# A two-layer graph network on one Trainium2 core: entries of 72 more tiles of adj gathered into the memory of x's later rows

## The chip, the core and the metric

The kernel runs on one NeuronCore of a Trainium2 chip. PE (TensorE) multiplies matrices, DVE (VectorE) and ACT (ScalarE) work on tiles of 128 partitions, POOL (GpSimd) does a few such operations and issues the gathers, that is, the DMAs whose rows are picked by a list of indices, and SP (SyncE) issues most of the other DMAs. Each engine runs its own instructions in the order in which they were written; between engines they wait on semaphores. The metric is the device time of one execution in microseconds (us); lower is better. Before the change it is 1088.14 us, the median of 4 runs (1078.37 to 1096.14).

## The reference

`x` has 2708 rows of 256, `adj` is 2708 by 2708, sparse, with entries of 0 or between 0.05 and 1 and a full diagonal. Two layers, each followed by an addition of `x` and a layer norm over the 256:

```python
# layer 0; h = x, node_adj = edge_adj = adj without its diagonal, dn = de = diag(adj)
node_support = adj @ h
edge_output = gru_cell(node_support, h, edge weights)
for each of 3 heads:
    hW = h @ W
    hp, hm = (adj > 0) @ hW, (adj < 0) @ hW
    e_plus, e_minus = leaky_relu([hp, hm] @ a), leaky_relu([hm, hp] @ a)
    att = softmax over j of (e_plus[j] where adj > 0, e_minus[j] where adj < 0, else -9e15)
    edge_support += (att * adj) @ hW / 3
node_output = gru_cell(edge_support, h, node weights)
x = layernorm(x + de * edge_output + dn * node_output)
# layer 1: an attention of 4 heads over the entries with adj > 0.5
h = x @ W
e = leaky_relu(s_src + s_dst) where adj > 0.5, else -1e9
x = layernorm(x + softmax(e) applied to h + bias)
```

## The kernel before

Few entries of adj are not zero, so layer 0 does not multiply by all of it. The kernel has three phases, all written in `fast_path` (line 305).

*The scan (0 to about 250 us).* adj, transposed, is read once, in 6 groups of 512 columns by 11 pairs of blocks of 128 rows (lines 853 to 920). For each pair SP loads a tile `at2` (one of four), ACT takes signs, POOL multiplies the pair's diagonal block by `off_diag` (line 887) where the pair holds it, DVE reduces which rows have an entry in each strip of 64 columns (`f_found`), and PE sums signs. Between the pairs go one or more of the `later` loads (line 718), which bring weights, x and table columns, and PE's `keep` products, parts of the cells worked out early and stored to `XH`. When a group is through, `listed` and `spread` (lines 538 and 592) write with DVE, ACT and PE the lists `idx0` of the rows that have entries, 128 to a tile.

*Layer 0 (about 250 to 905 us).* The loop at line 1205 goes over `work0`, 181 tiles of 128 rows by 64 columns: 163 gathered by list and 18 whole ones. Of its tiles 0 to 59 belong to the first group of 512 nodes, 60 to 94 to the second, 95 to 125 to the third, 126 to 149 to the fourth, 150 to 173 to the fifth, the rest to the last, which has 148 nodes. For each tile

- `fetch_raw` (line 662) gathers its entries of adj, 64 floats for each of 128 rows. The first `EARLY` = 40 tiles go to memory that `m1`, the masks of layer 1, takes later; the others go round the 32 places of `rawp`, which lie in `home4` (profile name `f_home`; other rings have homes of the same name);
- `fetch_rows` (line 951) gathers the same rows of the table `T0`, x and the exponents beside it, into one of nine tiles `rows`;
- `prepared` (line 970) makes from both the weighted entries `four` (DVE, then ACT), and after every eighth tile (`RAWS`) DVE takes the least entry of the eight, `low`, out of the memory they were gathered to;
- `multiplied` (line 1002) and `divided` multiply on PE and divide.

After a group's last tile come `cells_and_norm` (line 1070): the products with `gat_w` into `side`, copied by ACT; the two cells; `back` (line 1134), which adds the result to `xn`, x's rows in memory (22 blocks of 256 floats to a partition); the norm; and the write of layer 1's table `T1`. `fetch_mask` (line 1198) gathers the 91 masks of layer 1 into one of six `raw` tiles and converts each on DVE into `f_m`; the calls stand ahead of tile 40 and run when their lists are there.

*Layer 1 (from about 905 us)* gathers rows of `T1` and applies the masks.

x comes into `xn` by three `later` loads of seven blocks and one of 20 rows, and `T0`'s columns of x are written from `xn` by four more.

The order on each engine isn't the order of the lines. `fast_path` runs against a `Plan` (line 97) that notes each instruction with what it depends on (by the memory it touches) and a cost, for a gather 1.25 us on POOL and 3.0 until it lands (`cost`, line 149). `issue` (line 226) then takes, for the engine that is free first, the ready instruction with the longest chain of costs behind it, and that is the order in which they are written out. A change of memory changes the dependencies, and with them the order on every engine. All notes are made in one helper, so the profile has one line for all of them, L215, and its tables are read by the tiles' names.

Of the kernel before, what the change touches and what calls it, by code (L numbers as in the profile page):

```python
# [10 lines left out]
F32 = mybir.dt.float32  # L11
# [9 lines left out]
P = 128  # L21
D = 256
# [19 lines left out]
W0 = 64  # L42
# [262 lines left out]
def fast_path(ctx: ExitStack, tc: tile.TileContext, i: dict, out: bass.AP, bad: bass.AP):  # L305
# [11 lines left out]
    nc = plan = Plan(tc.nc)  # L317
    x, xT_in, adj, adjT = i["x"], i["xT"], i["adj"], i["adjT"]
    N = x.shape[0]
    NB = (N + P - 1) // P  # L320
    NF = N // P
    size = [min(P, N - b * P) for b in range(NB)]
    last = NB - 1
    GR = CH // P
# [20 lines left out]
    const = ctx.enter_context(tc.tile_pool(name="f_const", bufs=1))  # L345
# [18 lines left out]
    T0 = dram.tile([N, TW], F32, name="f_T0")  # L364
# [11 lines left out]
    home3 = const.tile([P, 4 * CH], F32, name="f_home3")  # L376
    home4 = const.tile([P, 4 * CH], F32, name="f_home4")
# [68 lines left out]
    for t, of in ((less_room, TILES0 + TILES1), (less_whole, WHOLE0 + WHOLE1)):  # L446
        c = 0
        while c < len(of):
            e = c
# [40 lines left out]
    def on_every(src, wide):  # L490
        return bass.AP(tensor=src.tensor, offset=src.offset, ap=[[0, P], [1, wide]])
# [20 lines left out]
    xn = const.tile([P, NB, D], F32, name="f_xn")  # L512
# [19 lines left out]
    nc.gpsimd.memset(flags1, 0.0)  # L532
    m1 = const.tile([P, sum(TILES1), W1], U8, name="f_m1")
    small, lists = Rings(const, 2), Rings(const, 2)
    hotp, rawp = Rings(const, 2, home3), Rings(const, 32, home4)


    def listed(layer, batch, made):
# [109 lines left out]
    def gathered(dst, table, idx, at):  # L648
        nc.gpsimd.indirect_dma_start(
            dst, None, table, bass.IndirectOffsetOnAxis(ap=idx, axis=0), element_offset=at  # L650
        )
# [4 lines left out]
            of += [(c, True, b) for b in range(whole[c])] + [(c, False, t) for t in range(room_of[c])]  # L656
    raws = {}

    EARLY = 40
    early = m1.rearrange("p t w -> p (t w)").bitcast(F32)[:, : EARLY * W0]  # L660

    def fetch_raw(n):

        c, whole, m = work0[n]
        d0, w = spans[0][c]
        raws[n] = early[:, n * W0 : n * W0 + w] if n < EARLY else rawp.tile([P, W0], F32, name="raw")[:, :w]
        if whole:
            nc.sync.dma_start(raws[n], adjT[m * P : (m + 1) * P, d0 : d0 + w])
        else:
            gathered(raws[n], adjT, idx0[:, c, m : m + 1], d0)  # L670
# [47 lines left out]
    def later(dst, src):  # L718
        loads.append(lambda: nc.sync.dma_start(dst, src))

    def later_kd(src, wide, name):
        t = const.tile([P, KD, wide], F32, name=name)
        later(t, src.rearrange("(k p) n -> p k n", p=P))
        return t
# [1 line left out]
    cells = []  # L726
    of_cells = ("edge", "node")
    w_hs = [later_kd(i[f"L0_gnn_{cell}_WhhT"], 3 * D, f"f_{cell}_wh") for cell in of_cells]
    for b in range(0, NF, 7):
        e = min(b + 7, NF)  # L730
        later(xn[:, b:e, :], x[b * P : e * P, :].rearrange("(b p) d -> p b d", p=P))
    if NF < NB:
        later(xn[: size[NF], NF, :], x[NF * P :, :])
    for cell, w_h in zip(of_cells, w_hs):
        w_i = later_kd(i[f"L0_gnn_{cell}_WihT"], 3 * D, f"f_{cell}_wi")
        b_i = const.tile([P, 3 * KD], F32, name=f"f_{cell}_bi")
# [8 lines left out]
    bias_b = const.tile([P, D], F32, name="f_bias_b")  # L745
    for t, name in ((as_b, "a_src"), (ad_b, "a_dst"), (bias_b, "bias")):
        later(t, on_every(i[f"L1_gnn_{name}"], D))
    for b in range(0, NF, 7):
        e = min(b + 7, NF)
        later(T0[b * P : e * P, :D].rearrange("(b p) d -> p b d", p=P), xn[:, b:e, :])  # L750
    if NF < NB:
        later(T0[NF * P :, :D], xn[: size[NF], NF, :])
    later(
        diag[:, :NF].rearrange("p (b o) -> p b o", o=1),
        bass.AP(tensor=adj.tensor, offset=adj.offset, ap=[[N + 1, P], [P * (N + 1), NF], [1, 1]]),
# [97 lines left out]
    for g, cs in enumerate(groups):  # L853
        w = width[g]
        pe, pf = accs[0], dbs[0]
        c0, nf = base[g] // W0, w // W0
        for b0 in range(0, NB, 2):
# [25 lines left out]
            for b in pair:  # L883
                if b in cs:
                    p, o = size[b], b * P - base[g]
# [16 lines left out]
            for b in pair:  # L902
                p = size[b]
# [3 lines left out]
            for b in pair:  # L907
                p = size[b]
# [53 lines left out]
    def of_rows(n):  # L962

        c, whole, m = work0[n]
        if c == 0 and whole:
            return xn[:, m, :], Ew[:, m, :HEADS0], E3[:, m, :]
        r = rows[n]
        return r[:, :D], r[:, D : D + HEADS0], r.bitcast(BF16)[:, 2 * (D + HEADS0) : 2 * (D + HEADS0) + H3]

    def prepared(n):  # L970

        c, whole, m = work0[n]
        d0, w = spans[0][c]
        raw = raws.pop(n)
        four = sp.tile([P, 4 * W0], F32, name="four")
        a = four[:, :w]
        own = d0 - m * P
        if not whole:
            nc.vector.scalar_tensor_tensor(
                a, iota[:, :w], rel0[:, c, m : m + 1], raw, op0=ALU.not_equal, op1=ALU.mult  # L980
            )
        elif 0 <= own < P:
            nc.vector.tensor_mul(a, raw, off_diag[:, own : own + w])
        else:
            nc.vector.tensor_copy(a, raw)
        weight = of_rows(n)[1]
        for h in range(HEADS0):
            nc.scalar.activation(four[:, (h + 1) * w : (h + 2) * w], a, AF.Copy, scale=weight[:, h : h + 1])
        m0 = sp.tile([P, W0], BF16, name="m0", bufs=2 * COUNTED)
        nc.scalar.activation(m0[:, :w], a, AF.Sign)  # L990

        if n % RAWS == RAWS - 1 or n == len(work0) - 1:
            k = n - n % RAWS
            of, at = (early, k) if k < EARLY else (home4, (k - EARLY) % 32)
            nc.vector.tensor_reduce(
                low[:, k // RAWS : k // RAWS + 1], of[:, at * W0 : (at + n - k + 1) * W0], AX.X, ALU.min
            )
        ready[n] = (four, m0)
# [71 lines left out]
    def cells_and_norm(g):  # L1070
        c0, w = base[g], width[g]
        cc = slice(c0, c0 + w)
        sa, z = zs[g]
        bl = groups[g]
# [59 lines left out]
        def back(b):  # L1134
            p = size[b]
            pt = side()
            for o in range(KD):
                nc.tensor.transpose(
                    pt[:p, o * P : (o + 1) * P], total[:, o, b * P - c0 : b * P - c0 + p], ident
                )  # L1140
            y = xn[:p, b, :]
            nc.vector.scalar_tensor_tensor(y, pt[:p, :D], diag[:p, b : b + 1], y, op0=ALU.mult, op1=ALU.add)
            stats(y, p, b)
# [14 lines left out]
        def projected(b):  # L1158
            p = size[b]
            ph = side()  # L1160
            for k in range(KD):
                nc.tensor.matmul(
                    ph[:p, : D + 2 * HEADS1], lhsT=xT[:, k, b * P : b * P + p], rhs=w1[:, k, :],
                    start=(k == 0), stop=(k == KD - 1),
                )
            nc.vector.tensor_copy(s_d[:p, b, :], ph[:p, D : D + 2 * HEADS1])
            ah = gp.tile([P, TW], F32, name="ah", bufs=2)[:p]
            of_head = ah[:, :H65].rearrange("p (h c) -> p h c", h=HEADS1)
            s = small.tile([P, 2 * HEADS1], F32, name="s_d")[:p]
            nc.vector.tensor_scalar(s, ph[:p, D : D + 2 * HEADS1], REACH1, -REACH1, op0=ALU.min, op1=ALU.max)  # L1170
            nc.scalar.activation(of_head[:, :, C1 :], s[:, :HEADS1].rearrange("p (h o) -> p h o", o=1), AF.Exp)
            nc.scalar.activation(ah[:, H65:], s[:, :HEADS1], AF.Exp, scale=SLOPE - 1.0)
            nc.tensor.transpose(pd[:HEADS1, b * P - c0 : b * P - c0 + p], s[:, HEADS1:], ident[:p, :p])
            nc.vector.tensor_mul(
                of_head[:, :, :C1], ph[:p, :D].rearrange("p (h c) -> p h c", h=HEADS1),
                of_head[:, :, C1:].to_broadcast([p, HEADS1, C1]),
            )
            nc.sync.dma_start(T1[b * P : b * P + p, :], ah)
        for b in bl:
            back(b)  # L1180
        rstds(bl)
# [4 lines left out]
        for b in bl:  # L1186
            projected(b)
# [17 lines left out]
    for n, (c, whole, m) in enumerate(work0):  # L1205
        if n == EARLY:
            for k in slot1:
                fetch_mask(k)
        fetch_raw(n)
        fetch_rows(n)  # L1210
        prepared(n)
        if multiplied(n):
            divided(c)
            d0, w = spans[0][c]
            if d0 + w in (base[g] + width[g] for g in range(NG)):
                cells_and_norm(d0 // CH)
# [140 lines left out]
def tile_adj_resnorm(tc: tile.TileContext, i: dict, out: bass.AP):  # L1357
    nc = tc.nc
    with tc.tile_pool(name="guard", bufs=1) as gp:
        bad = gp.tile([P, 1], F32, name="bad")  # L1360
        fast_path(tc, i, out, bad)
        with tc.tile_pool(name="guard_ps", bufs=1, space=PSUM) as ps:
            one = gp.tile([P, 1], F32, name="guard_ones")
            nc.vector.memset(one, 1.0)
            nc.vector.tensor_scalar(bad, bad, 0.0, None, op0=ALU.is_gt)
            n = ps.tile([1, 1], F32, name="n_bad")
            nc.tensor.matmul(n, lhsT=bad, rhs=one, start=True, stop=True)
            flag = gp.tile([1, 1], I32, name="flag")
            nc.vector.tensor_copy(flag, n)
        taken = nc.values_load(flag[0:1, 0:1], min_val=0, max_val=P)  # L1370
        with tc.If(taken > 0):
            general_path(tc, i, out)
# [436 lines left out]
```

## Time and profile before

| | |
|---|---|
| four runs, median | 1088.14 us |
| lowest, highest | 1078.37, 1096.14 us |
| profiled execution, its own time | 1079.45 us |
| its span, first to last instruction | 1077.4 us |
| busy: PE, DVE, ACT, POOL | 847.0 (79%), 616.4 (57%), 534.4 (50%), 521.5 us (48%) |
| mean granted clock of PE | 0.876 |
| DMA queues: hardware (SP), software (POOL), hardware (ACT) | 21.6%, 16.8%, 3.5% of 16 engines' span |

In the profile, a group of instructions is told by engine, operation and `out<-in` with the program's names. The number after `x` is how many there are, then busy time and the mean of one, then how long the engine stood idle before them and what ended most of that. The waits list for each engine what it waited for: us in total, times, the longest one. Busy shares are means over three phases with different limits, so the phase of a number matters. A gather counts as busy on POOL while POOL writes its descriptors, some 0.95 us; its data land later. The shares of the clock are of PE's full speed, as the throttle granted them.

### The profile page before, as it was taken

The page shows a single profiled execution, that of the slowest core. Times are in us where ns is not written, and L with a number is a line of the kernel's source. Part 1 is how long each engine was busy: PE and PEld are TensorE (multiplying, and loading weights), DVE is VectorE, ACT ScalarE, POOL GpSimd, SP SyncE. Part 2 cuts the span into 40 slices and gives each one's busy share as a digit, 9 for nine tenths or more (in the row PEclk, how much of TensorE's full clock was granted, in tenths as well). Part 3 has the DMA queues.
Part 4 walks back from the last instruction along what each step waited for, and adds up shares of the span by engine and source line. Part 5 has one row for each costly group of instructions (what it writes and reads, how often), then busy time and mean ns, then how long its engine had stood idle before and what let it go on. Part 6 is the DMA issues. An engine that isn't in the chain of part 4 may idle for free.

```text
span 1077.4 us, 13865 instructions
## 1 busy us (share of the span) xinstructions
PE 847.0 (79%) x3879; PEld 517.4 (48%) x3879; DVE 616.4 (57%) x2011; ACT 534.4 (50%) x1499; POOL 521.5 (48%) x613
## 2 busy tenths in 40 slices
PE   5983888898888777778977766988758886887783
PEld 3431333344666335553554335535523474776672
DVE  5772658842564248653753365347513545788897
ACT  4783778874777326562564244434602242034354
POOL 2054653003656737666765556466473301666650
PEclk9996979999988879799987988888888986899996
DMA  8983968764333224332533142232221101444433
GB/s 300 305 261 106 271 210 265 208 179 154 97 87 87 51 57 130 82 76 62 167 109 92 28 148 77 63 98 65 75 60 27 43 26 60 124 140 146 147 106 108
DMA packets 84302, 131.94 MB, mean 122 GB/s; under 512 B 21368, under 2 KB 43136, under 8 KB 83576
## 3 DMA queue, kind: packets, MB, share of 16 engines
q1 hardware_dynamic: 56056, 71.21, 21.6%
q0 software_dynamic: 20320, 45.59, 16.8%
q10 hardware_dynamic: 7840, 14.16, 3.5%
q8 instruction: 33, 0.54, 0.2%
q14 instruction: 53, 0.43, 0.1%
HBM read 109.79 MB, written 21.12 MB: 122 GB/s over the span
## 4 chain that ended last, share of the span: by engine, by line
PE 27%; DVE 11%; another core or an unknown queue 6%; issue 5%; ACT 2%; DMA 1%; POOL 0%; SPq 0%; DVEq 0%; POOLq 0%; ACTq 0%
PE side L215 14%; PE acc L215 9%; DVE f_home L215 7%; PE db L215 4%; DVE f_xn L215 2%; ACT four L215 1%; DVE st L215 1%; ACT f_home L215 1%; DMA rows<-f_T,f_idx 1%; DVE four L215 1%; DVE rden L215 0%; DVE rden_own L215 0%; DVE f_m L215 0%; ACT L215 0%
## 5 line engine op out<-in xcount | busy, mean ns | idle before, releaser
L215 POOL DMA_INDIRECT rows<-f_T,f_idx x254 | 254.4, 1002 | 254.8 <-issue 107.3
L215 PE MATMUL acc<-four,rows 128*128 128x256 f32 (+1 forms) x712 | 210.2, 439 | 15.1 <-ACT four L215 8.7
L215 PEld LDWEIGHTS acc<-four,rows 128*128 128x128 f32 x712 | 146.1, 217 | 56.2 <-issue 15.9
L215 ACT ACTIVATE four<-four,rows 128x64 f32<-128x64 f32 (+1 forms) x534 | 145.6, 336 | 40.7 <-DMA rows<-f_T,f_idx 12.1
L215 POOL DMA_INDIRECT f_home<-in_adjT_dram,f_idx x130 | 127.3, 979 | 57.0 <-issue 33.3
L215 POOL DMA_INDIRECT raw<-in_adj_dram,f_idx x91 | 89.4, 982 | 64.2 <-DVE f_m L215 39.6
L215 PE MATMUL acc<-f_home,rows 128*65 128x128 f32 (+1 forms) x480 | 68.1, 297 | 22.7 <-DVE f_home L215 18.7
L215 ACT ACTIVATE f_home<-f_home,f_minus_half 128x1024 bf16<-128x1024 f32 (+4 forms) x72 | 69.8, 976 | 26.1 <-remote 15.2
L215 DVE TENSOR_REDUCE f_found<-f_home 128x16 f32<-128x1024 f32 (+5 forms) x84 | 71.8, 883 | 16.0 <-DMA f_home<-in_adjT_dram 8.9
L215 PE MATMUL side<-f_home,f_edge_wi 128*128 128x512 f32 (+1 forms) x144 | 65.5, 597 | 19.4 <-DVE f_home L215 10.9
L215 DVE TENSOR_TENSOR f_home<-f_home,side 128x512 f32<-128x512 f32 (+1 forms) x56 | 36.7, 657 | 67.0 <-PE side L215 43.7
L215 ACT ACTIVATE f_home<-f_home 128x1024 bf16<-128x1024 f32 (+4 forms) x72 | 63.0, 882 | 17.8 <-PE acc L215 7.1
L215 PEld LDWEIGHTS acc<-f_home,rows 128*65 128x65 f32 x480 | 56.4, 149 | 30.9 <-DVE f_home L215 22.6
L215 DVE SCALAR_TENSOR_TENSOR four<-f_iota,f_rel,f_home 128x64 f32<-128x64 f32 (+1 forms) x130 | 35.6, 279 | 61.3 <-PE acc L215 22.9
L215 PE MATMUL side<-f_home,f_node_wi 128*128 128x512 f32 (+1 forms) x144 | 64.1, 580 | 4.8 <-DVE f_home L215 4.7
L215 PE MATMUL db<-f_home,f_only 128*22 128x512 bf16 (+2 forms) x132 | 40.7, 389 | 29.8 <-ACT f_home L215 26.6
L215 DVE SCALAR_TENSOR_TENSOR f_home<-pl,rows,f_m 128x128 f32<-128x128 f32 x196 | 55.0, 344 | 14.6 <-PE acc L215 5.7
L215 PE MATMUL side<-f_home,f_gat_w 128*128 128x512 f32 (+1 forms) x144 | 59.9, 575 | 1.5 <-DVE f_home L215 1.2
L215 PE MATMUL db<-f_home,rows 128*65 128x128 f32 x376 | 52.8, 291 | 7.3 <-DVE f_home L215 4.2
L215 PEld LDWEIGHTS side<-f_home,f_edge_wi 128*128 128x128 f32 x144 | 27.7, 205 | 53.3 <-issue 37.0
L215 ACT ACTIVATE m<-four 128x64 bf16<-128x64 f32 (+1 forms) x181 | 40.7, 246 | 19.0 <-DVE four L215 13.1
L215 PEld LDWEIGHTS db<-f_home,rows 128*65 128x65 f32 x376 | 43.5, 146 | 12.6 <-DVE f_home L215 6.7
(207 smaller groups left out, 1415.9 us busy)
## 6 DMA issues: line engine op xcount, KB each, us to landing
f_home<-in_adjT_dram SPq DMA_DIRECT2D x50, 512.0 KB
f_XH<-kept ACTq DMA_DIRECT2D x48, 256.0 KB
f_home<-f_XH SPq DMA_DIRECT2D x48, 256.0 KB
f_home<-f_TS SPq DMA_DIRECT2D x5, 1024.0 KB
rows<-f_T SPq DMA_DIRECT2D x31, 132.0 KB
rows<-f_T,f_idx POOLq DMA_INDIRECT x254
f_T<-f_home SPq DMA_DIRECT2D x21, 132.0 KB
f_xn<-in_x_dram SPq DMA_DIRECT2D x3, 896.0 KB
```

The source lines that it names most:

```text
L215: call = lambda: f(*args, **kwargs)
```

## The change

The ring `rawp` goes. A tile's entries now have a home by their number: the first 40 as before, the next 72 in `soon`, which is the memory of `xn`'s blocks 4 to 21 (18 blocks of 256 floats are 72 places of 64), and the others in turn in the 32 places of `home4`. The reduction `low` reads from the same home.

At the start only `xn`'s first four blocks are loaded; x's rows of the other groups are loaded in `cells_and_norm`, ahead of `back`, by SP (four loads of four blocks; for the last group one of a block and one of 20 rows). `T0`'s columns of x are copied from x in DRAM and no longer from `xn`.

```diff
-    hotp, rawp = Rings(const, 2, home3), Rings(const, 32, home4)
+    hotp = Rings(const, 2, home3)
...
-    EARLY = 40
+
+    EARLY, NEXT = 40, (NB - GR) * D // W0
     early = m1.rearrange("p t w -> p (t w)").bitcast(F32)[:, : EARLY * W0]
+    soon = xn[:, GR:, :].rearrange("p b d -> p (b d)")
+
+    def raw_home(n):
+
+        if n < EARLY:
+            return early, n
+        if n < EARLY + NEXT:
+            return soon, n - EARLY
+        return home4, (n - EARLY - NEXT) % 32
 
     def fetch_raw(n):
 
         c, whole, m = work0[n]
         d0, w = spans[0][c]
-        raws[n] = early[:, n * W0 : n * W0 + w] if n < EARLY else rawp.tile([P, W0], F32, name="raw")[:, :w]
+        home, at = raw_home(n)
+        raws[n] = home[:, at * W0 : at * W0 + w]
...
-    for b in range(0, NF, 7):
-        e = min(b + 7, NF)
-        later(xn[:, b:e, :], x[b * P : e * P, :].rearrange("(b p) d -> p b d", p=P))
-    if NF < NB:
-        later(xn[: size[NF], NF, :], x[NF * P :, :])
+    later(xn[:, :GR, :], x[: GR * P, :].rearrange("(b p) d -> p b d", p=P))
...
-    for b in range(0, NF, 7):
-        e = min(b + 7, NF)
-        later(T0[b * P : e * P, :D].rearrange("(b p) d -> p b d", p=P), xn[:, b:e, :])
-    if NF < NB:
-        later(T0[NF * P :, :D], xn[: size[NF], NF, :])
+    for b in range(0, NB, 7):
+        e = min((b + 7) * P, N)
+        later(T0[b * P : e, :D], x[b * P : e, :])
...
-            of, at = (early, k) if k < EARLY else (home4, (k - EARLY) % 32)
+            of, at = raw_home(k)
...
+        if g > 0:
+            full = [b for b in bl if size[b] == P]
+            if full:
+                nc.sync.dma_start(
+                    xn[:, full[0] : full[-1] + 1, :],
+                    x[full[0] * P : (full[-1] + 1) * P, :].rearrange("(b p) d -> p b d", p=P),
+                )
+            if len(full) < len(bl):
+                nc.sync.dma_start(xn[: size[last], last, :], x[last * P :, :])
         for b in bl:
             back(b)
```

## The prediction

> **What bounds the kernel now.** I read the page's chain first, then its groups, the waits by stage, the busy time by windows, and last the instructions around the longest gaps.
>
> ```profile
> PE 27%; DVE 11%; another core or an unknown queue 6%; issue 5%; ACT 2%; DMA 1%; POOL 0%; SPq 0%; DVEq 0%; POOLq 0%; ACTq 0%
> ...
> L215 POOL DMA_INDIRECT rows<-f_T,f_idx x254 | 254.4, 1002 | 254.8 <-issue 107.3
> ...
> L215 POOL DMA_INDIRECT f_home<-in_adjT_dram,f_idx x130 | 127.3, 979 | 57.0 <-issue 33.3
> L215 POOL DMA_INDIRECT raw<-in_adj_dram,f_idx x91 | 89.4, 982 | 64.2 <-DVE f_m L215 39.6
> ```
>
> PE leads the chain and POOL has 0% of it: the engine whose work this change moves is not the bound. POOL's work is gathers of about 0.98 us plus 0.30 us between two of them, 1.25 us each. The 130 into `f_home` and 33 into `f_m` are the entries of adj (the change concerns the 130), 91 into `raw` the masks of layer 1.
>
> Who waits for entries in layer 0 (250 to 905 us), by the waits of DVE, then of ACT:
>
> ```profile
> DVE f_low L215 <- DMA f_home<-in_adjT_dram,f_idx: 23.8, 4, 9.6
> ...
> DVE f_m L215 <- DMA raw<-in_adj_dram,f_idx: 21.6, 18, 3.4
> ```
>
> ```profile
> ACT four L215 <- DMA rows<-f_T,f_idx: 12.1, 12, 2.5
> ```
>
> The four `f_low` waits end at about 365.9, 497.1, 595.3 and 697.5 us. The last three lie in the gat_w products of a group's cells, where PE is busy without a break (10.0 of 10 us from 490, 590 and 690). They cost PE nothing.
>
> Then the windows. Columns: length, busy us (instructions) of PE, PE's weight loads, DVE, ACT, POOL, then PE's granted clock, DMA share and GB/s.
>
> ```profile
> 63.80:78.00 14.20, 10.91 (x62) 4.13 (x59) 9.74 (x14) 12.40 (x17) 11.10 (x11) 0.88 0.95 306
> 78.00:95.40 17.40, 3.68 (x22) 1.59 (x19) 0.00 (x0) 2.18 (x3) 13.17 (x14) 0.75 0.35 87
> 120.70:150.80 30.10, 24.53 (x81) 10.03 (x80) 20.92 (x41) 22.37 (x30) 23.64 (x22) 0.78 0.78 234
> 171.50:204.20 32.70, 29.56 (x139) 12.54 (x138) 27.62 (x56) 29.19 (x42) 0.00 (x0) 0.99 0.87 273
> 213.70:240.60 26.90, 26.90 (x123) 12.64 (x121) 13.40 (x40) 21.48 (x49) 0.00 (x0) 0.95 0.56 156
> ...
> 366.60:383.10 16.50, 8.07 (x17) 3.31 (x16) 0.03 (x1) 1.87 (x2) 12.54 (x14) 0.81 0.16 26
> ...
> 795.50:811.10 15.60, 0.01 (x1) 0.00 (x0) 1.15 (x5) 0.62 (x2) 8.45 (x9) 0.64 0.19 42
> ```
>
> Lines four and five: POOL has two empty stretches in the scan, 32.7 and 26.9 us. Lines two, six and seven: every engine but POOL nearly stands still. All three lie in the second half of a long unbroken train of gathers: 25 from 63.8 to 95.4, 24 from 352.7 to 383.1, 23 from 778.0 to 806.4. PE's longest gaps there are 17.9, 8.4 and 15.6 us. But 22 gathers from 120.7 to 150.8 (line three) cost PE only 2.8 us. Why such trains stop PE, the trace does not tell; that they go together is all I use. The third, on PE:
>
> ```profile
> 793.63 1.88 PE L215 MATMUL side<-f_home,f_edge_wi 128*128 128x512 f32 x4
> 811.10 3.78 PE L215 MATMUL side<-f_xT,f_edge_wh 128*128 128x512 f32 x4 [15.59 <-ACT f_home L215]
> ```
>
> The last line for later is on POOL, the first gather of T's rows after the last off_diag multiply:
>
> ```profile
> 240.63 0.63 POOL L215 TENSOR_TENSOR f_home<-f_home,f_off_diag 128x128 f32<-128x128 f32 x2 [26.96 <-ACT f_home L215]
> 250.53 0.98 POOL L215 DMA_INDIRECT rows<-f_T,f_idx  x1 [9.27 <-issue]
> ```
>
> **The change part by part.** All gathers stay (163 of entries, 91 masks, 254 of rows); the planner's order moves. I counted it in the two programs, on POOL.
>
> *Ahead of the first gather of rows:* 61 gathers of entries before, 108 after. 47 more at 1.25 us are 58.8 us; the two empty stretches hold 59.6 us. The lists decide when they can run. In the trace group 1's list is written at 158.3 and 164.5 us, group 2's at 195.2 and 202.9. After the change 26 gathers, which need no list later than group 1's, stand in one train between group 3's multiplies by off_diag (167.9 us) and group 4's first: 170.5 + 26 x 1.25 = 203 us, and that multiply ran at 205.7. Covered. Then 25 more stand between group 4's second multiply (212.8) and group 5's, for group 2's list: 213.7 + 25 x 1.25 = 245.0 us, where that multiply was ready at 240.6. PE's last products and the logits that the rows need queue behind it: **+4.4 us** on the path (nothing, if the 9.3 us before the first row gather swallow it; +10 if the lists slip by 5 us).
>
> *Trains in the scan.* The 26 and the 25 are two new unbroken trains. Price of one: from 2.8 us (the 22 at 120.7) to 17.9 us (the 25 at 63.8). By length they are nearest the second, by place and by work (a running scan whose lists of group 0 are done) nearest the first; I take the place: 2 x 2.8 = **+5.6 us**, bounds 0 and 35.8.
>
> *In the tile stretches of layer 0.* Up to the 150th gather of rows POOL has 102 gathers of entries and 43 masks before, 55 and 90 after: 145 against 145. The masks fill the room at once, so the stretches get no relief: ACT's 12.1 us for rows and the trains of 16 to 20 in the cells of groups 0 to 2 stay. 0 us, bounds -12.1 and +12.1. DVE's 23.8 us are worth 0 as shown; DVE will next wait there for masks (`f_m`, 21.6 us today).
>
> *Behind the 150th gather of rows* stood the other 48 masks; now one does. The train of 23 with 18 masks at 778.0 is gone, and with it, by my reading, the stop of PE: 15.6 us. What is late next there is ACT's copy of `side`, ready when the products end at 792. In the 5.9 us after the gap the clock was 0.5, so that work takes some 3 us less: **-18.6 us**, bounds -18.6 and 0.
>
> The clock row agrees with the Trainium skill, "TensorE: Matmul & The Clock Gate", section "Part 1: The HAM clock gate", that an idle window of about 3.4 us halves PE's clock; by that page's figure alone the regained work would be worth about half of one such window, 1.7 us, in place of my 3.
>
> *Loads of x.* Early on four loads (2.7 MB) become one of 0.5 MB, and T0's columns come from x directly: 2.25 MB less, at 304 GB/s (0 to 50 us) 7.4 us of DMA time. The 47 gathers read 47 x 32 KB = 1.5 MB more in the scan, in 16 packets of 2 KB and about 0.15 us each: 47 x 0.15 = 7.1 us over 16 engines. They balance: 0, bounds -7 and +7. T0's writes are complete by my reading well before 250 us.
>
> Six loads of xn (0.5 MB; 1.7 us at 304 GB/s, 4.3 us at the 122 GB/s of the whole span) enter SP's queue. They stand far ahead of the `back` that reads them; each waits for DVE's last read of those entries, and queued behind it are whole rows of T0, loads of XH and writes of T1. Had every one held its group by 4.3 us it would be 5 x 4.3 = 21 us; a group's cells last some 40 us, so I take 0.
>
> DVE: the same reductions `f_low`, six of them earlier, 0.68 us each, each behind eight landings. In the scan they stand in front of work on lists, but their gathers stand earlier still: 0, bounds 0 and 6 x 2.4 = 14 us (2.4 being the shortest such wait).
>
> One rule speaks against gathering beside a busy DVE. In 112 to 171 us DVE was busy two thirds of the time and gathers still took 0.94 us mostly, 0.97 to 0.98 in the mean, 2.38 at most. The Trainium skill, "SBUF — State Buffer", section "SBUF: two separate sides", says that POOL cannot write descriptors while DVE runs certain copies; from its 620 ns that become 3100 ns, an estimate for 47 gathers would be 47 x 2.5 = 117 us lost. The row decides: 0.
>
> Sum: 4.4 + 5.6 - 18.6 = **-8.6 us**. The profiled execution took 1079.45 us (span 1077.4), so 1070.9. It lies 8.7 us below the median 1088.14 of runs from 1078 to 1096; the same step from the median gives 1079.5. If the stops vary from run to run, the removed one is part of what separates them; I take a bit under the middle, **1074 us**.
>
> **The rivals.**
>
> *A. The stop at 778 goes and the scan stays whole (forecast).* 1070.9 less ACT's 12.1 and the 5.6 of the new trains, 1053, up to 1077. Chance 0.38.
>
> *B. The stop moves.* The masks that made the train of 23 now stand in trains of 17 to 20 in the cells of groups 0 to 3; before, such trains cost PE 8.4 (24), 4.1 (20), 3.3 (18), 2.4 (17). If three of them gain 6 each, the 18.6 are given back: 1088 + (4.4 + 5.6 + 18 - 18.6) = 1097, or about 1079 if none does. It says also that the promised relief does not happen, for which the count 145 against 145 speaks. 1077 to 1099. Chance 0.30.
>
> *C. Slower: the dense scan stops.* Place: the trains of 26 and 25, 170 to 245 us, where PE is at 29.6 of 32.7 and 26.9 of 26.9 us, so every microsecond counts. Price: 17.9 each as at 78 us, 35.8, + 4.4, and the stop at 778 returns half: 1079.45 + 35.8 + 4.4 - 9 = 1110.6. It decides from a total of 30 us of PE gap between 170 and 250. For it: length of train. Against it: 22 gathers at 120 to 150. Chance 0.32.
>
> **How the numbers follow.** About 1% is what a measurement of this kernel can tell from no change. A is faster by over 1% (below 1077), B within, C slower (above 1099): 0.38, 0.30, 0.32. A's own range is 1053 to 1077. The range for 8 in 10 takes A, B, and C to a little over its price: 1053 to 1112. Out of it are a scan that loses more than C's price, and gains from several terms at once.
>
> **What would show it.** Right: between 780 and 815 us no PE gap over 5 us, at most one mask behind row gather 150; POOL busy in 171 to 245; PE still at 27 and more of 30 us there; the first gather of rows at 250 to 257 us. Wrong: PE gaps over 8 us in 180 to 245 (C); new gaps of 8 us and more beside mask trains at 370 to 720 (B); `back` waiting for DMA of `f_xn`; POOL gathers with a mean over 1.1 us. Should the first row gather come before 245 us, the loads of x were worth more than I gave them; should it come after 265, the lists slipped.

## The result and the profile after

The changed kernel takes 1088.92 us (median of 10 runs, 1082.83 to 1097.28), the kernel before 1085.21 us in 15 runs taken with it (1066.75 to 1096.14). Ratios, here and below, leave out executions more than 1.5% above the fastest of the same kernel (nine of the 15 before), and three profiles of the experiments (loads alone, pauses in two places, pauses without the order) fell on such executions, so their rows are given but not compared closely. The ratio is 1.0152, 95% interval 1.0098 to 1.0206, while the two medians differ by 0.3%: the change makes the kernel no faster, and by the ratio some 1.5% slower. Its profiled execution took 1087.88 us (span 1086.1), against 1079.45 (1077.4).

The busy time by windows, as it was read before (length, then busy us of PE, its weight loads, DVE, ACT and POOL with instructions, PE's granted clock, DMA share, GB/s), now around the trains of gathers of the changed kernel (a train is an unbroken sequence of gathers on POOL):

```profile
68.30:85.60 17.30, 14.21 (x76) 5.59 (x72) 9.70 (x14) 13.19 (x18) 13.34 (x14) 0.90 0.89 263
85.60:106.40 20.80, 0.04 (x1) 0.08 (x1) 1.86 (x3) 2.68 (x4) 10.57 (x12) 0.62 0.14 27
...
175.60:198.70 23.10, 21.56 (x86) 8.62 (x86) 18.29 (x43) 18.58 (x23) 18.35 (x18) 0.93 0.94 259
198.70:209.30 10.60, 0.00 (x0) 0.00 (x0) 2.94 (x3) 3.26 (x4) 7.86 (x10) 0.71 0.40 92
230.10:251.70 21.60, 20.70 (x82) 9.08 (x80) 14.32 (x39) 13.66 (x25) 16.86 (x18) 1.00 0.64 181
251.70:263.30 11.60, 0.04 (x1) 0.09 (x1) 0.92 (x5) 0.93 (x2) 8.31 (x9) 0.61 0.23 53
...
824.10:839.70 15.60, 15.60 (x37) 6.84 (x36) 3.52 (x5) 3.10 (x6) 0.00 (x0) 1.00 0.00 0
```

Each pair of lines is one train: first all engines work, then nearly only POOL does. The train of 25 from 68.3 us was there before and stops PE for 20.8 us (17.9 before). The two new ones, from 175.6 and from 230.1 us, stop it for 10.6 and 11.6 us. The last line is the place in the program where PE stood still before, 13.8 to 29.4 us after the 163rd gather of rows (which came at 781.7 us before and comes at 810.3 now): PE works all of its 15.6 us, and POOL has nothing to do.

The waits of PE in the scan (50 to 262 us) put the same in one line, first of the kernel before, then of the changed one:

```profile
PE db L215 <- ACT f_home L215: 18.3, 2, 17.9
```

```profile
PE db L215 <- ACT f_home L215: 37.5, 5, 20.8
```

(Only waits that end by 262 us are in it, so the last gap isn't.) The end of the scan, on POOL:

```profile
276.94 0.98 POOL L215 TENSOR_TENSOR f_home<-f_home,f_off_diag 128x128 f32<-128x128 f32 x2 [14.49 <-ACT f_home L215]
287.23 0.98 POOL L215 DMA_INDIRECT rows<-f_T,f_idx  x1 [9.31 <-DMA f_T<-f_Ew]
```

The first gather of rows comes at 287.2 us and not at 250.5. So the balance, from the gathers of rows in the two profiles, is:

| stretch | before | after | difference |
|---|---|---|---|
| start to the 1st gather of rows (scan) | 250.5 | 287.2 | +36.7 |
| 1st to 163rd (tiles and cells of layer 0) | 531.2 | 523.1 | -8.1 |
| 163rd to 164th (end of layer 0) | 127.5 | 107.7 | -19.7 |
| 164th to the end of the span (layer 1) | 168.2 | 168.0 | -0.2 |

The sum is +8.7, the difference of the spans. The gathers themselves hardly changed:

```profile
L215 POOL DMA_INDIRECT f_home<-in_adjT_dram,f_idx x67 | 63.5, 948 | 27.1 <-issue 17.5
L215 POOL DMA_INDIRECT f_xn<-in_adjT_dram,f_idx x63 | 63.7, 1010 | 25.5 <-issue 17.9
```

The mean of one is 948 and 1010 ns where it was 979. The question is what made the scan 37 us longer.

### The profile page after: what moved, and what is told of

It is laid out like the page before. It is cut to its first block, busy times and chain, and to the rows that moved or that the text cites. A ratio compares the mean times of both kernels' runs of the same rounds, so it can differ in the third digit from the quotient of the medians.

```text
span 1086.1 us, 13831 instructions
## 1 busy us (share of the span) xinstructions
PE 843.7 (78%) x3879; PEld 513.4 (47%) x3879; DVE 612.7 (56%) x2011; ACT 535.9 (49%) x1499; POOL 528.7 (49%) x613
## 5 line engine op out<-in xcount | busy, mean ns | idle before, releaser
L215 POOL DMA_INDIRECT rows<-f_T,f_idx x254 | 258.7, 1018 | 293.7 <-issue 146.8
L215 PE MATMUL acc<-four,rows 128*128 128x256 f32 (+1 forms) x712 | 206.3, 433 | 31.8 <-ACT four L215 19.5
L215 PEld LDWEIGHTS acc<-four,rows 128*128 128x128 f32 x712 | 142.9, 213 | 73.7 <-ACT four L215 25.4
L215 POOL DMA_INDIRECT raw<-in_adj_dram,f_idx x91 | 93.0, 1021 | 57.5 <-DVE f_m L215 32.7
L215 POOL DMA_INDIRECT f_home<-in_adjT_dram,f_idx x67 | 63.5, 948 | 27.1 <-issue 17.5
L215 POOL DMA_INDIRECT f_xn<-in_adjT_dram,f_idx x63 | 63.7, 1010 | 25.5 <-issue 17.9
L215 PE MATMUL side<-f_home,f_node_wi 128*128 128x512 f32 (+1 forms) x144 | 60.0, 548 | 1.5 <-DVE f_home L215 1.4
L215 PE MATMUL side<-f_home,f_gat_w 128*128 128x512 f32 (+1 forms) x144 | 57.3, 555 | 1.2 <-DVE f_home L215 1.2
L215 PE MATMUL db<-f_home,rows 128*65 128x128 f32 x376 | 48.4, 278 | 5.8 <-DVE f_home L215 5.5
L215 PE MATMUL acc<-f_home,f_home 128*9 128x512 bf16 (+2 forms) x132 | 42.2, 404 | 10.3 <-ACT f_home L215 9.4
```

Source lines behind the costliest of these rows:

```text
L215: call = lambda: f(*args, **kwargs)
```

## The experiments

Three causes are at hand for the scan: the new loads of x, the gathers' place in POOL's queue (the multiplies by `off_diag` behind them), and the stop of the other engines while a long train runs. "Gathers ahead" below counts gathers of entries in front of the first gather of rows.

**The loads of x alone** (`e1_loads`): the kernel before with the change's early load of four blocks, the copies into T0 and the late loads, but with the ring.

```diff
-        later(xn[:, b:e, :], x[b * P : e * P, :].rearrange("(b p) d -> p b d", p=P))
...
+    later(xn[:, :GR, :], x[: GR * P, :].rearrange("(b p) d -> p b d", p=P))
...
+        later(T0[b * P : e, :D], x[b * P : e, :])
...
+        if g > 0:
+            full = [b for b in bl if size[b] == P]
```

> The kernel before with only the change's loads of x: the first four blocks of xn early, the others ahead of back, T0's columns copied from x. The ring of 32 places stays, so 61 gathers of entries stand ahead of the first gather of rows as before. Theory (the long trains of gathers stop the scan): the first gather of rows comes within 5 us of the 250.5 us of before, the ratio to the kernel before is 0.99 to 1.01, and the stop at 778 is still there. Rival (the loads of x slow the scan, for which the first list came 4.5 us later in the changed kernel): the first gather of rows comes after 262 us and the ratio is 1.01 or more.

Measured: 1082.40 us against 1083.16, ratio 1.0025 (0.9973 to 1.0078). By the time, the loads cost nothing that can be told (the interval ends at +0.8%, some 8 us). The stop behind the 163rd gather of rows is still there, with a PE gap of 14.4 us. In the profile the first gather of rows came at 263.6 us, past the 262 that was to speak for the loads; the next run, which has the loads too, decides.

**The gathers held until the scan is over** (`e2_hold`):

```diff
+    nc.vector.tensor_copy(
+        soon.rearrange("p (n w) -> p n w", w=W0)[:, :, :1],
+        found0[:, len(TILES0) - 1, NB - 1 :].rearrange("p (n o) -> p n o", o=1).to_broadcast([P, NEXT, 1]),
+    )
     for n, (c, whole, m) in enumerate(work0):
```

> The changed kernel in which a DVE copy of 72 elements, which needs the last group's found rows, stands ahead of the gathers into xn's later rows, so that they can't run in the scan: 48 gathers of entries stand ahead of the first gather of rows (108 in the changed kernel). Theory (trains): the first gather of rows comes at 240 to 256 us where the changed kernel has 287; the gathers come back in layer 0, which takes as long as before or longer, and the masks stand at its end again; ratio to the kernel before 0.99 to 1.015. Rival (the loads of x): the first gather of rows stays after 270 us.

Measured: first gather of rows at 250.2 us, time 1087.14, ratio 1.0079 (1.0038 to 1.0121). With the loads of x in place and the gathers out of the scan, the 37 us are gone. They came with the gathers. Layer 0 (1st to 164th gather of rows) then takes 661.2 us, as long as before (658.7) and longer than in the changed kernel (630.8), as expected: a train of 25 in a group's cells stops PE for 16.9 us at 496.8.

**Pauses in the trains of the scan** (`e3_fill`). POOL multiplies a spare tile six times after every fourth gather in a row. The planner counts the time, so the order changes a little.

```diff
             for call in op.calls:
                 call()
+            if e == "gpsimd":
+                run = run + 1 if op.method == "indirect_dma_start" else 0
...
+                rows += op.out.startswith("rows")
+                if run >= 4 and rows == 0:
+                    run, free[e] = 0, free[e] + 2.4000000000000004
+                    for _ in range(6):
+                        self.fill()
...
+    spare = const.tile([P, 100], F32, name="f_spare")
...
+    plan.fill = lambda: tc.nc.gpsimd.tensor_mul(spare, spare, spare)
```

> The changed kernel in which, until the first gather of rows, POOL does six small multiplies on a spare tile (some 2 us) after every fourth gather in a row, so that no train is longer than four; 88 gathers of entries stand ahead of the first gather of rows. Theory (a long unbroken train stops the other engines): no PE gap over 8 us between 60 and 250 us, where the changed kernel has 20.8, 10.6 and 11.6, and the first gather of rows comes 15 to 35 us before the 287 us of the changed kernel. Rival (POOL's time itself, its queue, delays the scan): POOL now has 40 us more work in the scan, the gaps stay, and the first gather of rows comes at 287 us or later.

Measured: 1061.24 us, ratio 0.9816 (0.9757 to 0.9875), first gather of rows at 244.3 us. The multiplies add 47 us of POOL work up to there; as 20 gathers fewer stand there, POOL is busy for 162.1 us in place of 130.6, and the scan became 43 us shorter. The longest PE gap between 50 and 250 us is 5.3 us. So the queue on POOL is not what made the scan of the changed kernel long: it became fuller. In the longest gap of the changed kernel ACT doesn't wait for POOL either ("remote": the profile names no engine); in the 5.3 us that are left here it does, for the multiply by `off_diag` behind gathers and pauses. First the changed kernel, then this one:

```profile
103.72 1.15 ACT L215 ACTIVATE f_home<-f_home,f_minus_half 128x1024 bf16<-128x1024 f32 x1 [19.03 <-remote]
```

```profile
102.44 1.06 ACT L215 ACTIVATE f_home<-f_home 128x1024 bf16<-128x1024 f32 x1 [5.16 <-POOL f_home L215]
```

**Pauses in the last train of the kernel before** (`e4_fill`, the same edit with `159 <= rows <= 163`, on the kernel before).

> The kernel before in which the same filling work stands after every fourth gather in a row between the 159th and the 163rd gather of rows, that is in the train of 23 at 778 us with its 18 masks and in the masks behind it. Nothing else moves. Theory (the train makes the stop): the PE gap of 15.6 us falls below 5 us, the time from the 163rd to the 164th gather of rows falls from 127.5 to some 110 us as in the changed kernel, and the ratio is 0.98 to 0.99. Rival (the stop has another cause, such as a wait of the cells): the gap stays over 10 us and the ratio is 1.00.

Measured: 1062.66 us, ratio 0.9772 (0.9694 to 0.985). The 163rd to the 164th gather of rows takes 111.0 us. The window around the old stop, of this kernel:

```profile
785.00:830.00 45.00, 45.00 (x106) 19.84 (x106) 17.18 (x42) 10.76 (x20) 35.73 (x59) 1.00 0.15 40
```

PE works 45.00 of 45 us where it stood still for 15.6, and the clock is 1.00 throughout. As before, 39 masks are gathered between the 163rd and the 164th gather of rows, and PE's order of instructions in this window is that of before; the pauses are new.

**A break without a pause** (`e5_tiny`): one multiply of one column, 0.21 us in the profile, after every fourth gather of the changed kernel's scan.

> The changed kernel in which, until the first gather of rows, POOL does one multiply of a single column (some 0.1 us) after every fourth gather in a row; 107 gathers of entries stand ahead of the first gather of rows. It parts the train without giving it time. Theory 1 (an unbroken sequence of gathers is what stops PE, any other instruction frees it): as with the filling of 2 us, no PE gap over 8 us between 60 and 260 us, and the time is near 1061 us. Theory 2 (the rate of the gathers is what stops PE, and the filling helped by its time): the PE gaps of 20, 10 and 11 us come back, the first gather of rows stays after 270 us, and the ratio to the kernel before is 1.00 to 1.02.

Measured: 1085.75 us, ratio 1.0063 (1.0028 to 1.0098), first gather of rows at 268.9 us, PE gaps of 9.6 and 7.3 us. It lies between the two theories and by the time nearer to the second: a break of 0.21 us shortens the gaps and brings the first gather of rows 18 of the 37 us back in this profile, but the time gains nothing that can be told.

**The same pauses in smaller steps** (`e9_pairs`, three multiplies after every second gather).

> The changed kernel with three multiplies (some 1.2 us) after every second gather in a row until the first gather of rows, in place of six after every fourth: the same mean pitch of about 1.85 us, in smaller steps; 84 gathers of entries stand ahead of the first gather of rows. If the mean rate of the gathers is what stops PE, the time is that of the filling by fours, 1061 us (1053 to 1069), with no PE gap over 8 us in the scan. If the pauses have to be 2 us long, gaps over 8 us are back and the time is above 1070.

Measured: 1059.50 us, ratio 0.979 (0.9627 to 0.9953), first gather of rows at 240.0 us, no PE gap over 5.5 us in the scan. At one mean rate of the gathers, the length of the single pause makes no difference that can be told (1061.24 us with six after four).

**Pauses everywhere, and how long** (`e7_after_all`, `e10_after_half`, `e12_after_third`: the changed kernel with six, three and two multiplies after every fourth gather of entries or masks, scan and layer 0).

> The changed kernel with the filling of six multiplies after every fourth gather of entries or masks in a row, in all of the scan and layer 0; 88 gathers of entries stand ahead of the first gather of rows. Theory (long trains cost PE 5 to 8 us each in the groups' cells too): PE gaps over 6 us in 340 to 780 us vanish and the time is 1035 to 1055 us. Rival (POOL is full in layer 0, so the filling's 2 us delay the gathers of rows): the waits for rows and entries grow, and the time is 1061 us or more.

> The changed kernel with three multiplies (some 1.2 us) after every fourth gather of entries or masks in a row in the scan and layer 0, a mean pitch of about 1.55 us between the 1.25 of the changed kernel and the 1.85 of the full filling; 104 gathers of entries stand ahead of the first gather of rows. If the stops grow with the rate, PE gaps of 5 to 10 us remain and the time lies between 1030 and 1086, near 1050. If there is a threshold below 1.55 us, the time is 1030 or less, since POOL works less on filling.

> The changed kernel with two multiplies (some 0.8 us) after every fourth gather of entries or masks in a row, a mean pitch of about 1.45 us; 107 gathers of entries stand ahead of the first gather of rows. If the stops set in with the rate, gaps of PE over 8 us come back and the time lies over 1020; if 0.8 us after four are enough, it is 1000 to 1010 us.

Measured: 1030.36 us (ratio 0.9544, 0.9465 to 0.9623) with six, 1010.00 (0.9375, 0.9284 to 0.9465) with three, 1023.31 (0.953, 0.946 to 0.9601) with two. Three are best of these. Six did 5 us better than its range (1035 to 1055); three fell into the case of a threshold (1030 or less); two fitted neither case that was expected, since no PE gap in the scan exceeds 4 us, as with three, and the time is still 13 us longer. Of the kernel with three, the waits of PE in the scan begin with

```profile
PE acc L215 <- ACT f_home L215: 5.7, 9, 2.8
...
PE db L215 <- ACT f_home L215: 2.5, 2, 2.1
```

the last in place of the 37.5 us above, with 104 gathers ahead (108 in the changed kernel) and the first gather of rows at 237.6 us.

**The change with and without, once nothing stops PE** (`e6_before_all`, `e8_before_two`, `e11_before_half`: the kernel before with six multiplies everywhere, with six in the scan and the last masks alone, and with three everywhere).

> The kernel before with the filling of six multiplies after every fourth gather of entries or masks in a row, in all of the scan and layer 0; 61 gathers of entries stand ahead of the first gather of rows. Against the changed kernel so filled (1030 us, 88 gathers ahead) it shows what the change is worth when no train stops PE. If its 27 further gathers in the scan save their time in layer 0, this one takes 1040 us or more; if they only move work, 1025 to 1035; if they cost the scan (it ended at 240 us with 61 and at 251 with 88), 1015 to 1025.

> The kernel before with the filling of six multiplies after every fourth gather in the scan and in the last masks of layer 0; 61 gathers of entries stand ahead of the first gather of rows as before. If the two stops (17.9 us at 81.7 and 15.6 at 795.5) are all that the filling takes away, the time is 1083 less 15 to 18 and less 15 to 20, some 1050 us, ratio 0.965 to 0.975, and the change's 47 further gathers in the scan are then worth nothing once the trains are parted (the changed kernel so filled in the scan has 1061 and no stop at the end). If the further gathers are worth something, this one isn't faster than 1061.

> The kernel before with three multiplies after every fourth gather of entries or masks in a row in the scan and layer 0, as in the changed kernel of 1010 us with this filling; 61 gathers of entries stand ahead of the first gather of rows (104 there). If the change's further gathers in the scan are worth their POOL time in layer 0 once no train stops PE, this one takes 1020 to 1035 us; if they are worth nothing, 1010 or less.

Measured: 1040.99 us (0.9676, 0.9549 to 0.9804) with six, 1060.05 (0.9789, 0.9694 to 0.9884) in two places, 1006.61 (0.9356, 0.9295 to 0.9417) with three. At three multiplies the kernel before is at 0.9356 and the changed one at 0.9375: the same, as expected if the gathers moved are worth nothing. At six the changed one is ahead, 0.9544 against 0.9676, with intervals that overlap; there the kernel before loses its time behind the 164th gather of rows, 184.8 us where the changed one has 168.0. At three multiplies the first gather of rows comes at 232.4 us with 61 gathers ahead and at 237.6 with 104, and layer 0 (1st to 164th gather of rows) takes 598.3 and 598.1 us. So the 43 gathers more cost the scan 5 us and save layer 0 nothing once no train stops PE: what the change was to bring is at most small. The sum expected of two places (1050) was missed by 10 us; the two gains do not simply add, and why is not shown.

**Order or pauses** (`e13_order`, `e14_fill`). The planner counts the pauses and so writes another order. One kernel has the order of the 1010 us kernel without the multiplies, the other the changed kernel's own order with them (the edit is that of the second, against the 1010 us kernel):

```diff
-                    run, free[e] = 0, free[e] + 1.2000000000000002
+                    run = 0
                     for _ in range(3):
                         self.fill()
```

> The changed kernel in the order of the one with three multiplies after every fourth gather (1010 us), planned with their time, but without the multiplies themselves: the gathers run one behind the other again. If the pauses on POOL make the gain, the time is 1070 to 1095 us with PE gaps over 8 us beside the trains; if the planner's other order makes it, 1005 to 1020 us.

> The changed kernel in its own order on every engine, with the three multiplies added on POOL after every fourth gather of entries or masks in a row and not counted in the plan. If the pauses make the gain, the time is 1005 to 1030 us and the first gather of rows comes before 250 us where the changed kernel has 287; if the order makes it, 1080 us or more.

Measured on one chip, where the kernel before took 1093.62: the order alone 1087.89 us (ratio 0.9986, 0.9942 to 1.0031), the pauses alone 1053.82 (four runs, 1037.95 to 1058.24; the medians' ratio is 0.964, without an interval). Busy time in the same 210 us of the scan (50 to 260 us), first of the changed kernel, then of the pauses alone, then of the 1010 us kernel:

```profile
50.00:260.00 210.00, 145.59 (x640) 58.50 (x639) 116.02 (x256) 131.21 (x181) 113.23 (x126) 0.85 0.66 192
```

```profile
50.00:260.00 210.00, 168.58 (x726) 69.71 (x725) 126.31 (x292) 145.63 (x222) 148.78 (x197) 0.87 0.70 203
```

```profile
50.00:260.00 210.00, 180.72 (x824) 80.89 (x823) 134.18 (x318) 157.57 (x268) 156.82 (x205) 0.92 0.74 218
```

POOL does 36 to 44 us more in it, and PE does 23 to 35 us more as well. The first gather of rows comes at 258.3 us with the pauses alone, 29 us before the changed kernel's. The order gains nothing by itself (PE gaps of 16.2 and 10.9 us stand beside its trains); with the pauses it gains further. Both expectations for the pauses alone, 1005 to 1030 us and a first gather of rows before 250, were missed. One PE gap of 10.2 us is left in its scan, and it is POOL's queue: ACT waits for the multiply by `off_diag`, which comes at 107.8 us and in the 1010 us kernel at 98.2:

```profile
108.68 1.06 ACT L215 ACTIVATE f_home<-f_home 128x1024 bf16<-128x1024 f32 x1 [10.06 <-POOL f_home L215]
```

So a plan that knows of the pauses is part of the 1010.

## Why the prediction was wrong

The forecast was 1074 us, faster by 1.3%; the kernel became no faster, and by the ratio 1.5% slower. That 1088.92 us lies inside the stated range, and inside rival B's too, is luck: the forecast's scan was 27 us too short, and what B describes did not happen. The sum promised -8.6 us; the spans of the two profiles give +8.7. Step by step:

- **The trains in the scan, +5.6 us: this step failed.** For two trains of 26 and 25 the price lay between 2.8 (a train of 22 in the same stage) and 17.9 us (a train of 25 a stage earlier), and the prediction took the first, because of the place. The two stopped PE for 10.6 and 11.6 us, 22.2 in place of 5.6. The rest of the scan's +36.7 is a first train that begins 4.5 us later (68.3 against 63.8), its stop of 20.8 for 17.9, and gaps of 5.7 us at 154.7 (in place of the 2.8) and of 4.6 at 215; these make 37 together. With the pauses on POOL in place and the order on every engine unchanged, the first gather of rows comes 29 us earlier; with a plan that counts the pauses, 50.
- **Rival C** had the right mechanism, and a sign named for it came, a PE gap over 8 us between 180 and 245. Its sum for the scan, 35.8 + 4.4 = 40.2, lies within 4 us of 36.7, but by luck: the two trains cost 22.2 and not 35.8, the multiply cost nothing, and the rest came from gaps that it didn't name. Its other sign, 30 us of PE gap between 170 and 250, was not reached (10.6 and 4.6; the third gap begins at 251.7). Neither row, by place or by length, gave the price; it lay about halfway.
- **The multiply behind the last train, +4.4 us**: not so. POOL was idle for 14.5 us before it and waited for ACT. The lists and signs were late because PE, DVE and ACT had stood still, not because POOL's queue was full.
- **The stop at 778, -18.6 us**: right in mechanism and size. From the 163rd to the 164th gather of rows 19.7 us are saved, and the pauses in that train alone (127.5 to 111.0) show that the train made it. (It held 19 masks behind four gathers of rows; the prediction counted 18.)
- **The tile stretches, 0 us**: measured -8.1, inside the bounds. ACT's waits for rows fell from 12.1 to 9.8 us only, and DVE's for entries from 23.8 to 15.7 (over 280 to 918 us, the same stage), which the prediction had found to cost PE nothing. PE's longest waits between 262 and 780 us other than the scan's last gap are 8.4, 8.4, 6.9 and 6.0 us before and 7.9, 4.8 and 4.6 after; that would be enough for the 8.1, but no run isolates it.
- **The loads of x, 0 us**: right by the time (1.0025, interval 0.9973 to 1.0078). Whether they are the 4.5 us by which the first train comes later is not shown.
- **The loads into `xn` ahead of `back`, DVE's earlier reductions**: no group waits for `f_xn` from x in the profile; one reduction waits 6.4 us for its gathers in the scan, inside the bound of 14.
- **That gathers beside a busy DVE are not slower**: right. The 63 into `f_xn`, all in the scan, took 1010 ns in the mean, 940 at least and 944 at the median, where the 130 before took 979 in the mean and 944 at the median. The rule in the Trainium skill, "SBUF — State Buffer", section "SBUF: two separate sides", that DVE can keep POOL from writing descriptors, had no visible part here; what the runs show is the other direction, POOL's gathers and the engines beside them.
- **The clock**: its mean in the three gaps was 0.62, 0.71 and 0.61. The Trainium skill, "TensorE: Matmul & The Clock Gate", section "Part 1: The HAM clock gate", has the clock at half after an idle window of about 3.4 us; means between a half and one over gaps of 10.6 to 20.8 us fit that. It follows from the stops and does not make them, since PE has nothing to run in them.

Rival B, the stop moving into the cells, is not what happened: the gaps there are 7.9 us and less.

## What to carry to other kernels

When a queue of gathers is off the chain, ask not only whether it fits into idle time but how densely it runs: here most trains of twenty and more gathers, 1.25 us apart, stopped every other engine, and moving work into POOL's empty stretch made such trains. When two rows bound a cost and lie far apart, find what differs between them before choosing one; here the price lay between them. A gap that appears on all engines at once beside one that is busy is worth an experiment of its own: 0.4 us multiplies on a spare tile, three after every four gathers, took some 6% off a tuned kernel, far more than the change was meant to.

## What the runs showed that was not expected

While POOL issues gathers at 1.25 us each, PE, DVE, ACT and SP run on for some 14 to 23 us and then nearly stop until about the end of the train (in one case PE resumes 4 us before it; gaps of PE of 20.8, 10.6 and 11.6 us; 16.9 in the kernel with held gathers). More POOL work in the same stretch, if it is not gathers, makes them run again. In the profile the stop looks like a circle: PE waits for ACT, and ACT for a signal that the profile puts down to no engine. In the kernel before, ACT copies `side` at 810.47 us after 19.07 us of waiting, where the products that it copies end at 792 in PE's records:

```profile
810.47 0.58 ACT L215 COPY f_home<-side 128x512 f32<-128x512 f32 x1 [19.07 <-remote]
```

Why the signals come late is open; no run here looks inside. Open too is why 22 gathers at 120 us cost only 2.8 us, and why two multiplies in place of three cost 13 us though the long gaps are gone (in the profiles, 10.9 us apart, 5.1 of it lie in the scan and 3.8 between the 163rd and the 164th gather of rows). Of the kernels tried, those with three multiplies after every fourth gather are the fastest: 1006.61 us on the kernel before and 1010.00 on the changed one, both well ahead of the 1080 to 1094 of the kernel before.
